# Prices, hops and search width of a static instruction planner in a four-layer graph network kernel

## The chip, the cores and the metric

The kernel runs on one core of one Trainium2 chip, in 32-bit floats. The metric is the device time of one execution in microseconds (us); the time before is 2462.25 us, the median of three runs (2461.93 to 2463.06). The engines are TensorE (PE, with its weight loads as PEld), VectorE (DVE), ScalarE (ACT), GpSimd (POOL) and SyncE (SP), each with its own queue of instructions that it works off in order.

## The reference

128 graphs of 64 nodes with 256 features pass through four layers. Each adds a graph layer's output to its input and normalises over the features:

```python
def _L0_gnn_ref(x, adj, mask, weight, w_ih, w_hh, b_ih, b_hh):    # gated graph layer, 5 rounds
    A = (adj != 0).astype(x.dtype)
    h = x
    for l in range(weight.shape[0]):
        m = jnp.einsum('bnd,de->bne', h, weight[l])
        agg = jnp.einsum('bij,bid->bjd', A, m)
        h = _gru_cell(agg, h, w_ih, w_hh, b_ih, b_hh)
    return h * mask[..., None]

def _L1_gnn_ref(x, adjacency, epsilon, W1, b1, rms_weight, W2, b2):
    agg = epsilon * x + jnp.einsum('bnm,bmd->bnd', adjacency, x)
    h = jnp.einsum('bnd,dh->bnh', agg, W1) + b1
    h = jax.nn.silu(_rmsnorm(h, rms_weight))
    return jnp.einsum('bnh,hd->bnd', h, W2) + b2

def _L2_gnn_ref(x, adj):                                          # on the hyperbolic ball
    x_tangent = logmap0(x)
    support_t = jnp.einsum('bij,bjd->bid', adj, x_tangent)
    return project(expmap0(support_t))

def _L3_gnn_ref(hidden, mask, W_w, W_b, a_w, a_b):                # attention
    h = jnp.einsum('bnd,ed->bne', hidden, W_w) + W_b
    ...
    return jnp.einsum('bnm,bmd->bnd', a, h)

x = _layernorm(x + _L0_gnn_ref(x, adj, nodemask, ...), axis=-1)
x = _layernorm(x + _L1_gnn_ref(x, adj, ...), axis=-1)
x = _layernorm(x + _L2_gnn_ref(x, adj), axis=-1)
x = _layernorm(x + _L3_gnn_ref(x, adj, ...), axis=-1)
```

## The kernel before

The work is cut into 16 groups of 8 graphs. A group's code does not emit its instructions at once: it hands each one to a planner, with the engine, an estimated duration (its price) and what it reads and writes. A group is one stream of operations. When all 16 are listed, the planner plays the engines against the prices and chooses in which order the operations of up to four streams go into each engine's queue; only that order reaches the chip. The prices themselves never do: on the chip each instruction starts when its engine is free and its inputs are there.

An operation as the planner holds it, and the step that advances one plan: it takes, again and again, the operation that can start first, and among equals the one a rule prefers. Marks `...` stand for cuts.

```python
    def advance(self, until, rank):
        flow, need, at, clock, banks = self.flow, self.need, self.at, self.clock, self.banks
        while self.left and clock["PE"] < until:
            best = None
            for s in range(self.first, min(self.first + flow.WINDOW, len(self.queues))):
                for e, q in self.queues[s].items():
                    opened = False
                    for _, o in zip(range(flow.AHEAD[e]), q):
                        t = max(clock[e], at[o.id])
                        if o.opens is not None:
                            if opened or not banks or need[o.id]:
                                opened = True
                                continue
                            t = max(t, banks[0])
                        elif need[o.id]:
                            continue
                        elif o.kb and e != "POOL":
                            t = max(t, self.lands[0])
                        key = (t, *rank(s, o))
                        if best is None or key < best[0]:
                            best = key, o
            if best is None:
                return False
            t, o = best[0][0], best[1]
            self.queues[o.stream][o.eng].remove(o)
            self.order.append(o)
            end = t + o.us
            clock[o.eng] = end
            if o.eng == "PE":
                self.done += o.us
            if o.opens is not None:
                banks.pop(0)
            for b in o.bufs:
                n = self.uses.get(b, b.left) - 1
                self.uses[b] = n
                if not n:
                    banks.append(end + flow.hop(o.eng, "PE"))
                    banks.sort()
            if o.kb:
                self.bus = max(self.bus, end + flow.DMA[0]) + o.kb / flow.DMA[1]
                end = self.bus + flow.DMA[2]
                if o.eng != "POOL":
                    self.lands = [*self.lands[1:], end]
            for u in o.then:
                need[u.id] -= 1
                at[u.id] = max(at[u.id], end + flow.hop(o.eng, u.eng))
            self.left -= 1
            while self.first < len(self.queues) and not any(self.queues[self.first].values()):
                self.first += 1
        return True

    def bound(self):

        now = self.clock["PE"]
        end = max(now - self.done + self.flow.work, *self.clock.values())
        for q in self.queues[self.first:]:
            for d in q.values():
                if d:
                    end = max(end, max(self.at[d[0].id], now) + d[0].way)
        return end
```

The rules of play, the hops (time from the end of an operation to the start of one that needs it on another engine) and the search over plans:

```python
    AHEAD = {"PE": 32, "DVE": 10, "ACT": 10, "POOL": 4, "SP": 2}
    HOPS = {"from PE": 0.25, "to PE": 0.3, "else": 0.1}
    DMA = (2.0, 330.0, 1.0)
    TRANSFERS = 8
    WINDOW, STRETCH, WIDTH, LAG = 4, 25.0, 8, 40.0
    ...
    def hop(self, e, to):
        if e == to:
            return 0.0
        return self.HOPS["from PE" if e == "PE" else "to PE" if to == "PE" else "else"]

    def ways(self):

        for i, o in enumerate(o for s in self.streams for o in s):
            o.id = i
        path = {}
        for ops in self.streams:
            longest = 0.0
            for o in reversed(ops):
                path[o] = o.us + max((path[u] + self.hop(o.eng, u.eng) for u in o.then if u.stream == o.stream), default=0.0)
                o.way = longest = max(longest, path[o])
        self.work = sum(o.us for ops in self.streams for o in ops if o.eng == "PE")

    def issue(self):
        self.ways()
        ranks = (lambda s, o: (s, o.n), lambda s, o: (s if o.kb else -s, o.n), lambda s, o: (self.LAG * s - o.way, s, o.n))
        plans, until = [Plan(self)], 0.0
        while any(p.left for p in plans):
            until += self.STRETCH
            found = {}
            for p in plans:
                for rank in ranks:
                    c = p.copy()
                    if c.advance(until, rank):
                        found.setdefault((round(c.bound(), 3), c.left), c)
            plans = [found[k] for k in sorted(found)[:self.WIDTH]]
        p, parts = plans[0], []
        past = (p.past, p.order)
        while past is not None:
            parts.append(past[1])
            past = past[0]
        ...   # the operations are emitted in the order of the best plan
```

The prices, by engine:

```python
    def pe(n, run, w, r):
        flow.op("PE", {512: 0.86, 256: 0.435, 128: 0.23, 1: 0.21}.get(n, 0.3), run, w, r)

    def turn(run, w, r):
        flow.op("PE", 0.11, run, w, r)

    def dve(n, run, w, r):
        flow.op("DVE", 0.16 + 0.00105 * n, run, w, r)

    def act(n, run, w, r):
        flow.op("ACT", 0.27 + 0.00077 * n, run, w, r)

    def pool(us, run, w, r=()):
        flow.op("POOL", us, run, w, r)
```

What the last groups do after their five gated rounds, cut to the operations that the profile shows at the end. The normalisation, used four times by each group:

```python
            st, mv = tiny("st", (P, NB, 6)), tiny("mv", (P, NB, 2))
            ve, rstd = tiny("ve", (P, 2, NB)), tiny("rstd", (P, 2, NB))
            for b in range(NB):
                dve(256, lambda b=b: nc.vector.bn_stats(st[:, b, :], y[:, b, :]), [(st, b)], [(y, b)])
                dve(4, lambda b=b: nc.vector.bn_aggr(mv[:, b, :], st[:, b, :]), [(mv, b)], [(st, b)])
            m = 2 if norm else 1
            dve(4, lambda: nc.vector.tensor_tensor(
                ve[:, :m, :], over(mv[:, :, 1], m), eps2[:, :m, :], OP.add), [ve], [mv])
            pool(1.1, lambda: nc.gpsimd.tensor_tensor(rstd[:, :m, :], ve[:, :m, :], pow2[:, :m, :], OP.pow), [rstd], [ve])
            if norm:
                dve(4, lambda: nc.vector.scalar_tensor_tensor(
                    norm.tile(), rstd[:, 1, :], float(np.sqrt(D)), rstd[:, 0, :], OP.mult, OP.mult), [norm], [rstd])
            o = rows(tag, f"x_{name}")
            off = tiny("off")
            dve(4, lambda: nc.vector.scalar_tensor_tensor(
                off.tile(), mv[:, :, 0], -1.0, rstd[:, 0, :], OP.mult, OP.mult), [off], [mv, rstd])
            for b in range(NB):
                if b % 2:
                    act(300, lambda b=b: nc.scalar.activation(
                        o[:, b, :], y[:, b, :], AF.Identity, bias=off[:, b:b + 1], scale=rstd[:, 0, b:b + 1]),
                        [(o, b)], [(y, b), off, rstd])
                else:
                    dve(240, lambda b=b: nc.vector.tensor_scalar(
                        o[:, b, :], y[:, b, :], mv[:, b, 0:1], rstd[:, 0, b:b + 1], OP.subtract, OP.mult),
                        [(o, b)], [(y, b), mv, rstd])
            return o
```

From the gated rounds to the second layer's output (the first line turns the state into rows; `ps_hid` and `ps_o1` are the two large products):

```python
        for n in range(2):
            ps = rows_of(hT, n)
            ...                                   # y0 = rows * nodemask + x
        x1 = layer_norm(y0, "A", "n0")
        for n in range(2):
            aggregate(aggm, x1, 2 * n, n)
        ...
        for c in range(KH):
            ps = bank("ps_hid")
            ...                                   # two 512-wide matmuls; hid and sq on ACT, sqs on DVE
        ps = bank("ps_ss")
        ...                                       # row sums of squares on PE, power on POOL, ps_rms on PE
        for c in range(KH):
            hc = hid[c]

            dve(512, lambda hc=hc, c=c: nc.vector.scalar_tensor_tensor(
                hc[0][:, hc[1], :], hc[0][:, hc[1], :], rmsc(c), ps_r.tile(), OP.mult, OP.mult), [hc], [hc, ps_r, cols])
            th = u("VZR"[c % 3], f"th{c}")
            act(512, lambda hc=hc, th=th: nc.scalar.activation(th.tile(), hc[0][:, hc[1], :], AF.Tanh, scale=0.5),
                [th], [hc])
            dve(512, lambda hc=hc, th=th: nc.vector.scalar_tensor_tensor(
                hc[0][:, hc[1], :], th.tile(), 1.0, hc[0][:, hc[1], :], OP.add, OP.mult), [hc], [hc, th])
        y1 = xb
        for h in range(NB // 2):
            ps = bank("ps_o1")
            ...                                   # 32 matmuls 256 wide for each half, y1 on DVE
        xn = tiny("n")
        x2 = layer_norm(y1, "A", "n1", xn)
```

The third and fourth layer:

```python
        ...
        act(2600, lambda: nc.scalar.activation(fac.tile(), fac.tile(), AF.Ln), [fac], [fac])
        ...                                       # a series of 9 small DVE operations, then the factor
        tan = rows("B", "tan")
        ...                                       # four scalings on DVE, ps_sup on PE, squares on ACT
        ...                                       # power on POOL, tanh on ACT, 6 small DVE operations
        x3 = layer_norm(y2, "B", "n2")
        for n in range(2):
            feats_of(x3T, x3, n)                  # ps_T: transposes on PE, copy on ACT
        ...                                       # ps_a: 258-wide matmuls, exp and scale on ACT
        ...                                       # ps_att on PE, four small steps each on DVE
        o = layer_norm(y3, "A", "n3")
        flow.op("SP", 0.1, lambda: nc.sync.dma_start(out_rows[g], o.tile()), (), [o])
```

## Time and profile before

| what | before |
|---|---|
| time, median of 3 runs | 2462.25 us |
| span of the profiled execution | 2460.1 us |
| TensorE busy | 2418.4 us (98%) |
| VectorE busy | 1708.3 us (69%) |
| ScalarE busy | 1232.9 us (50%) |
| GpSimd busy | 181.1 us (7%) |
| mean granted TensorE clock | 0.994 of full speed |
| data read and written | 24.69 and 8.39 MB |

The span runs from the first to the last instruction of one execution taken by the hardware profiler; the time of a run is some 2 us longer. An engine's busy time is the sum of the stretches in which it worked on at least one instruction; matmul ends are modelled, so a busy TensorE is not TensorE at its peak. A 32-bit matmul shows as two records. A wait line reads: engine, tile and line, what released it, then total us, how often, and the longest. In the order of time each row is a run of like instructions, with the idle time ahead of it in brackets.

### The profile page before, as it was taken

What the parts mean: (1) busy time and instruction counts of PE and PEld (TensorE: products, weight loads), DVE (VectorE), ACT (ScalarE), POOL (GpSimd) and SP (SyncE); (2) the same over time, 40 slices, a digit from 0 to 9 for tenths busy, and PEclk for the clock granted to TensorE, in tenths of its full rate; (3) what the DMA queues carried; (4) which work ended last, traced back from release to release, by engine and by line L of the source; (5) the groups of instructions that cost most, each with busy time, mean ns of one, the idle gap of its engine ahead of it and who ended that gap; (6) DMA issues with size and microseconds to landing.
All of it is one profiled execution on the core that took longest, in us unless ns stands there. A gap on an engine that the chain in (4) does not pass through costs nothing.

```text
span 2460.1 us, 31915 instructions
## 1 busy us (share of the span) xinstructions
PE 2418.4 (98%) x11922; PEld 2045.9 (83%) x11922; DVE 1708.3 (69%) x3741; ACT 1232.9 (50%) x2612; POOL 181.1 (7%) x144
## 2 busy tenths in 40 slices
PE   9999999999999999999999999999999999999995
PEld 7887887878788887888878788788888878878864
DVE  3656776767777766776776777677676767856776
ACT  3445455454545545454554544555554554454453
POOL 4000000000000000000000000000000000000011
PEclk9999999999999999999999999999999999999997
DMA  4000000000000000000000000000000000000000
GB/s 126 2 2 10 1 26 3 1 29 1 28 1 29 1 18 11 1 29 1 18 12 1 28 1 26 3 15 15 1 29 1 1 29 1 27 1 1 10 17 17
DMA packets 39145, 35.11 MB, mean 14 GB/s; under 512 B 9892, under 2 KB 38592, under 8 KB 38992
## 3 DMA queue, kind: packets, MB, share of 16 engines
q1 hardware_dynamic: 37264, 31.20, 4.0%
q8 instruction: 94, 1.54, 0.3%
q10 hardware_dynamic: 1328, 1.31, 0.2%
q0 software_dynamic: 400, 0.57, 0.1%
q14 instruction: 59, 0.48, 0.1%
HBM read 24.69 MB, written 8.39 MB: 13 GB/s over the span
## 4 chain that ended last, share of the span: by engine, by line
PE 73%; DVE 3%; ACT 1%; POOL 0%; issue 0%; POOLq 0%; ACTq 0%; DVEq 0%
PE p_v L625 9%; PE p_w L625 8%; PE p_r L625 8%; PE p_in L625 8%; PE p_hn L625 8%; PE ps_o L322 8%; PE ps_hid L322 8%; PE ps_agg L322 5%; PE p_u L625 4%; PE ps_hr L605 2%; PE ps_a L322 2%; PE ps_sup L322 1%; PE ps_att L322 1%; PE ps_T L595 1%; PE ps_ss L322 0%; DVE st L635 0%
## 5 line engine op out<-in xcount | busy, mean ns | idle before, releaser
L625 PE MATMUL p_hn<-hT,w_hn 128*128 128x256 f32 x1280 | 321.0, 380 | 0.1
L625 PE MATMUL p_in<-agg,w_in 128*128 128x256 f32 x1280 | 312.9, 380 | 0.0
L625 PEld LDWEIGHTS p_in<-agg,w_in 128*128 128x128 f32 x1280 | 241.5, 190 | 31.5 <-issue 0.5
L625 PEld LDWEIGHTS p_hn<-hT,w_hn 128*128 128x128 f32 x1280 | 229.4, 191 | 26.6 <-issue 2.6
L322 PE MATMUL ps_o<-w2s,hid 128*128 128x256 f32 x1024 | 230.0, 380 | 1.5 <-DVE hid L853 1.3
L322 PE MATMUL ps_hid<-aggm,w1s 128*128 128x512 f32 x512 | 224.1, 593 | 0.1
L322 PEld LDWEIGHTS ps_o<-w2s,hid 128*128 128x128 f32 x1024 | 194.3, 191 | 28.5 <-DVE hid L853 2.4
L640 POOL TENSOR_TENSOR rstd<-ve,pow 128x4 f32<-128x4 f32 (+1 forms) x64 | 81.9, 1280 | 1577.6 <-DVE ve L638 1569.3
L322 PEld LDWEIGHTS ps_hid<-aggm,w1s 128*128 128x128 f32 x512 | 96.7, 190 | 111.2 <-issue 108.3
L618 ACT COPY agg<-ps_agg 128x512 f32<-128x512 f32 x160 | 93.5, 584 | 149.2 <-PE ps_agg L322 123.1
L729 ACT ACTIVATE V<-V,half_b 128x256 f32<-128x256 f32 x160 | 73.0, 501 | 183.8 <-DVE V L725 183.7
L694 ACT ACTIVATE hnb<-p_hn,half_b 128x256 f32<-128x256 f32 x320 | 135.8, 471 | 55.7 <-PE p_hn L625 53.7
L625 PE MATMUL p_w<-tA,s 128*128 128x256 f32 x640 | 160.7, 380 | 0.0
L625 PE MATMUL p_v<-tB,s 128*128 128x256 f32 x640 | 159.5, 380 | 0.0
L625 PE MATMUL p_u<-tA,s 128*128 128x256 f32 x640 | 155.5, 380 | 1.5 <-DVE tA L708 1.4
L625 PE MATMUL p_w<-hT,s 128*128 128x256 f32 x640 | 156.7, 380 | 0.0
L625 PE MATMUL p_v<-tB,na 128*128 128x256 f32 x640 | 154.7, 380 | 0.7 <-DVE V L725 0.7
L625 PE MATMUL p_r<-hT,a 128*128 128x256 f32 x640 | 155.2, 380 | 0.2
L625 PE MATMUL p_r<-agg,a 128*128 128x256 f32 x640 | 154.1, 380 | 0.0
L833 DVE TENSOR_TENSOR sqs<-sqs,sq 128x512 f32<-128x512 f32 x112 | 77.4, 691 | 104.7 <-ACT sq L830 104.5
L322 PEld LDWEIGHTS ps_agg<-edge,hr 128*128 128x128 f32 x1024 | 137.3, 192 | 8.5 <-issue 1.4
L322 PE MATMUL ps_agg<-edge,hr 128*128 128x128 f32 x1024 | 139.1, 275 | 0.0
(205 smaller groups left out, 4435.3 us busy)
## 6 DMA issues: line engine op xcount, KB each, us to landing
x<-in_x_dram SPq DMA_DIRECT2D x16, 512.0 KB, 3.5
xr<-in_x_dram SPq DMA_DIRECT2D x16, 512.0 KB, 3.5
out_dram<-x_n SPq DMA_DIRECT2D x16, 512.0 KB, 2.9
edge<-in_adj_dram SPq DMA_DIRECT2D x32, 64.0 KB, 2.3
wm<-in_L_gnn_weight_dram SPq DMA_DIRECT2D x5, 256.0 KB, 4.9
w1s<-in_L_gnn_W_dram SPq DMA_DIRECT2D x1, 1024.0 KB, 6.3
w2s<-in_L_gnn_W_dram SPq DMA_DIRECT2D x1, 1024.0 KB, 10.0
aw_in_L_gnn_w_hh_dram<-in_L_gnn_w_hh_dram ACTq DMA_DIRECT2D x1, 512.0 KB, 5.6
```

What stands on the lines that cost most here:

```text
L322: return nc.tensor.matmul(o, lhsT, rhs, start=(k == 0), stop=(k == nk - 1))
L595: turn(lambda j=j, c=c: nc.tensor.transpose(ps[:, c * HR + j * P:c * HR + (j + 1) * P], src[:, 2 * n + j, c * P:(c + 1) * P], ident.tile() ...
L605: turn(lambda j=j, c=c: nc.tensor.transpose(ps[:, j * D + c * P:j * D + (c + 1) * P], src[:, c, (2 * n + j) * P:(2 * n + j + 1) * P], iden ...
L618: act(512, lambda: nc.scalar.copy(dst[:, :, half(n)], blocks_of(ps.tile())), [(dst, n)], [ps])
L625: pe(256, lambda c=c, k=k: nc.tensor.matmul(ps[:, c * HR:(c + 1) * HR], w[:, k, c * P:(c + 1) * P], v(k), start=first and c == k == 0, sto ...
L640: pool(1.1, lambda: nc.gpsimd.tensor_tensor(rstd[:, :m, :], ve[:, :m, :], pow2[:, :m, :], OP.pow), [rstd], [ve])
L694: act(300, lambda c=c: nc.scalar.activation(hnb[:, c, half(n)], p_hn[:, c * HR:(c + 1) * HR], AF.Identity, bias=half_b[:, 2 * KD + c:2 * K ...
L729: act(256, lambda c=c: nc.scalar.activation(o[:, c, :], src(c), AF.Tanh, bias=half_b[:, i * KD + c:i * KD + c + 1], scale=0.5), [(o, c)], ...
L833: dve(512, lambda sq=sq: nc.vector.tensor_add(sqs.tile(), sqs.tile(), sq.tile()), [sqs], [sqs, sq])
```

## The change

Only the planner's numbers and its search change. The prices of DVE, ACT and POOL operations are set anew, in good part per operation instead of by one formula, from durations seen in a trace. The hops become a part after the giving engine and a part before the taking one, and now also count between two dependent operations of one engine other than PE. An operation may hand over its result `early`, before its engine is free: the logarithm, whose price holds the reload of the tanh table that follows. In the last stretch of the span (`ENDGAME`, 350 us of planned TensorE work) the search goes in steps half as long and keeps three times as many plans. It is meant to make the planned course agree with the real one and to search the end more closely. The computation, the buffers and the transfers stay as they are.

```diff
-                at[u.id] = max(at[u.id], end + flow.hop(o.eng, u.eng))
+                at[u.id] = max(at[u.id], end + flow.hop(o, u.eng))
...   (cut)
-    HOPS = {"from PE": 0.25, "to PE": 0.3, "else": 0.1}
+    AFTER = {"PE": 0.2, "DVE": 0.12, "ACT": 0.13, "POOL": 0.04, "SP": 0.5}
+    BEFORE = {"PE": 0.1, "DVE": 0.0, "ACT": 0.0, "POOL": 0.05, "SP": 0.1}
+    ENDGAME = 350.0
...   (cut)
-    def op(self, eng, us, run, w=(), r=(), kb=0):
-        o = Op(eng, us, run, len(self.streams) - 1, len(self.ops), kb)
+    def op(self, eng, us, run, w=(), r=(), kb=0, early=0.0):
+        o = Op(eng, us, run, len(self.streams) - 1, len(self.ops), kb, early)
...   (cut)
-    def hop(self, e, to):
-        if e == to:
-            return 0.0
-        return self.HOPS["from PE" if e == "PE" else "to PE" if to == "PE" else "else"]
+    def hop(self, o, to):
+        return 0.0 if o.eng == to == "PE" else self.AFTER[o.eng] + self.BEFORE[to] - o.early
...   (cut)
-            until += self.STRETCH
+            late = until > self.work - self.ENDGAME
+            until += self.STRETCH / 2 if late else self.STRETCH
-            plans = [found[k] for k in sorted(found)[:self.WIDTH]]
+            plans = [found[k] for k in sorted(found)[:self.WIDTH * (3 if late else 1)]]
...   (cut)
-        flow.op("DVE", 0.16 + 0.00105 * n, run, w, r)
-    def act(n, run, w, r):
-        flow.op("ACT", 0.27 + 0.00077 * n, run, w, r)
+        flow.op("DVE", 0.075 + 0.00105 * n, run, w, r)
+    def act(us, run, w, r, early=0.0):
+        flow.op("ACT", us, run, w, r, early=early)
...   (cut)
-            act(512, lambda: nc.scalar.copy(dst[:, :, half(n)], blocks_of(ps.tile())), [(dst, n)], [ps])
+            act(0.49, lambda: nc.scalar.copy(dst[:, :, half(n)], blocks_of(ps.tile())), [(dst, n)], [ps])
...   (cut)
-            pool(1.1, lambda: nc.gpsimd.tensor_tensor(rstd[:, :m, :], ve[:, :m, :], pow2[:, :m, :], OP.pow), [rstd], [ve])
+            pool(1.65 if norm else 1.1, lambda: nc.gpsimd.tensor_tensor(rstd[:, :m, :], ve[:, :m, :], pow2[:, :m, :], OP.pow), [rstd], [ve])
...   (cut)
-                    act(300, lambda b=b: nc.scalar.activation(
+                    act(0.5, lambda b=b: nc.scalar.activation(
-                    dve(240, lambda b=b: nc.vector.tensor_scalar(
+                    dve(236, lambda b=b: nc.vector.tensor_scalar(
...   (cut)
-                    act(512, lambda: nc.scalar.copy(hr[:, 2 * n:2 * n + 2, :], blocks_of(ps.tile())),
+                    act(0.49, lambda: nc.scalar.copy(hr[:, 2 * n:2 * n + 2, :], blocks_of(ps.tile())),
-                    act(300, lambda c=c: nc.scalar.activation(
+                    act(0.375, lambda c=c: nc.scalar.activation(
...   (cut)
-                    act(256, lambda c=c: nc.scalar.activation(
+                    act(0.4, lambda c=c: nc.scalar.activation(
...   (cut)
-                    act(256, lambda c=c: nc.scalar.activation(t[:, c, :], t[:, c, :], AF.Tanh, bias=bih(2 * KD + c)),
+                    act(0.4, lambda c=c: nc.scalar.activation(t[:, c, :], t[:, c, :], AF.Tanh, bias=bih(2 * KD + c)),
...   (cut)
-            act(420, lambda: nc.scalar.copy(uu.tile(), blocks_of(p1.tile())), [uu], [p1])
+            act(0.49, lambda: nc.scalar.copy(uu.tile(), blocks_of(p1.tile())), [uu], [p1])
...   (cut)
-                dve(256, lambda ps=ps, b=b, j=j, blk=blk: nc.vector.scalar_tensor_tensor(
+                dve(300, lambda ps=ps, b=b, j=j, blk=blk: nc.vector.scalar_tensor_tensor(
...   (cut)
-            act(512, lambda ps=ps, hc=hc, c=c: nc.scalar.activation(
+            act(0.59, lambda ps=ps, hc=hc, c=c: nc.scalar.activation(
...   (cut)
-            act(512, lambda hc=hc, th=th: nc.scalar.activation(th.tile(), hc[0][:, hc[1], :], AF.Tanh, scale=0.5),
+            act(0.535, lambda hc=hc, th=th: nc.scalar.activation(th.tile(), hc[0][:, hc[1], :], AF.Tanh, scale=0.5),
...   (cut)
-        act(2600, lambda: nc.scalar.activation(fac.tile(), fac.tile(), AF.Ln), [fac], [fac])
+        act(2.67, lambda: nc.scalar.activation(fac.tile(), fac.tile(), AF.Ln), [fac], [fac], 1.28)
...   (cut)
-                act(450, lambda b=b, j=j, ps=sup[h]: nc.scalar.activation(
+                act(0.48, lambda b=b, j=j, ps=sup[h]: nc.scalar.activation(
-        act(64, lambda: nc.scalar.activation(th.tile(), unb.tile(), AF.Tanh), [th], [unb])
+        act(0.11, lambda: nc.scalar.activation(th.tile(), unb.tile(), AF.Tanh), [th], [unb])
...   (cut)
-        dve(800, onto_ball, [th, un], [th, un, urn])
+        dve(900, onto_ball, [th, un], [th, un, urn])
-            dve(256, lambda b=b, ps=sup[b // 2]: nc.vector.scalar_tensor_tensor(
+            dve(300, lambda b=b, ps=sup[b // 2]: nc.vector.scalar_tensor_tensor(
...   (cut)
-            act(4, lambda ps=ps, b=b: nc.scalar.activation(
+            act(0.17, lambda ps=ps, b=b: nc.scalar.activation(
-            act(256, lambda ps=ps, b=b: nc.scalar.activation(
+            act(0.38, lambda ps=ps, b=b: nc.scalar.activation(
...   (cut)
-            dve(256, lambda ps=ps, b=b: nc.vector.scalar_tensor_tensor(
+            dve(300, lambda ps=ps, b=b: nc.vector.scalar_tensor_tensor(
...   (cut)
```

## The prediction

> **What bounds the kernel now.** I read the page's busy table first, then the waits of TensorE (PE), then the busy time by stretches of the span, then the order of time at the end.
>
> ```profile
> span 2460.1 us, 31915 instructions
> PE 2418.4 (98%) x11922; PEld 2045.9 (83%) x11922; DVE 1708.3 (69%) x3741; ACT 1232.9 (50%) x2612; POOL 181.1 (7%) x144
> ```
>
> PE is busy for all but 2460.1 - 2418.4 = 41.7 us. No reordering of the same instructions can save more than these and what a lower clock costs. The waits of PE say what ended its idle time (total, times, longest, in us):
>
> ```profile
> PE ps_T L595 <- DVE x_n L654: 12.7, 2, 10.1
> PE ps_sup L322 <- DVE tan L900: 5.1, 1, 5.1
> PE ps_x L448 <- POOL ident masks.py:199: 2.5, 1, 2.5
> PE ps_ss L322 <- DVE sqs L833: 1.9, 1, 1.9
> ```
>
> These are single long waits, not many small ones. The stretches show where they lie (length, then busy us of PE, weight loads, DVE, ACT, POOL; then PE's granted clock, DMA share, GB/s):
>
> ```profile
> 800.00:1200.00 400.00, 399.01 (x1981) 339.78 (x1980) 284.21 (x614) 205.18 (x433) 24.17 (x18) 1.00 0.03 9
> 1200.00:1600.00 400.00, 400.00 (x1983) 339.01 (x1982) 283.10 (x601) 203.87 (x426) 25.22 (x18) 1.00 0.04 14
> 2300.00:2350.00 50.00, 50.00 (x240) 40.53 (x239) 39.86 (x91) 26.98 (x58) 5.61 (x3) 1.00 0.07 22
> 2350.00:2400.00 50.00, 43.42 (x170) 30.01 (x168) 34.58 (x82) 26.61 (x45) 7.38 (x5) 0.97 0.03 11
> 2400.00:2420.00 20.00, 14.14 (x59) 11.56 (x59) 15.19 (x53) 6.31 (x17) 3.21 (x3) 0.91 0.00 0
> 2420.00:2440.00 20.00, 9.47 (x36) 7.18 (x35) 16.63 (x74) 9.93 (x25) 2.63 (x3) 0.76 0.00 0
> 2440.00:2461.00 21.00, 8.36 (x32) 6.81 (x32) 8.75 (x34) 6.74 (x16) 2.01 (x2) 0.66 0.15 51
> ```
>
> From 2350 on PE is idle for 6.6 + 5.9 + 10.5 + 11.7 = 34.7 us (the last stretch is listed 0.9 us past the span's end). At the start it waits 2.5 us for the identity; the 2300 us between hold only some 4 us. So the middle is TensorE-bound almost without gaps, and the end is bound by the chain of small operations of the last two groups: PE has nothing else left to do. The order of time there, PE only (start, duration, what, idle before and its releaser):
>
> ```profile
> 2354.04 0.60 PE L605 MATMUL ps_hr<-ident,hT 128*128 128x128 f32 x4
> 2356.53 1.05 PE L322 MATMUL ps_ss<-ones,sqs 128*128 128x1 f32 x8 [1.89 <-DVE sqs L833]
> ...
> 2402.79 3.46 PE L322 MATMUL ps_sup<-tan,adjT 128*128 128x256 f32 x8 [5.10 <-DVE tan L900]
> ...
> 2428.46 1.47 PE L322 MATMUL ps_att<-hw,adjT 128*128 128x257 f32 x6
> 2440.01 1.94 PE L595 MATMUL ps_T<-ident,x_n 128*128 128x128 f32 x8 [10.08 <-DVE x_n L654]
> 2441.77 4.87 PE L322 MATMUL ps_a<-wattT,x3T 128*128 128x258 f32 x16
> 2446.47 1.90 PE L322 MATMUL ps_att<-hw,adjT 128*128 128x257 f32 x8
> ```
>
> The reader sees the last group alone from 2430 on: a hole of 10.1 us, three short pieces on PE, and from 2448.4 to 2460.1 no PE work at all (the last normalisation and the output transfer).
>
> **A floor.** Start-to-start in dense stretches gives PE's real work: 0.216 us for an instruction 256 wide (eight p_w in 1.73), 0.429 for 512, 0.111 for an aggregation of 128, 0.109 for a transpose. The groups by shape count 8616, 552, 1536 and about 1090 of these, and 128 of the sums' 0.1: 1861 + 237 + 170 + 119 + 13 = 2400 us. With 2.5 ahead of the first matmul and 11.7 behind the last, 2414 us is the least that any order gives; the span is 46 above it.
>
> **What the Trainium skill says.** "TensorE: Matmul & The Clock Gate", Part 1 (The HAM clock gate): after an idle window of about 3.4 us the array falls to half clock and needs as long a busy window to come back. The trace agrees: the clock column falls from 1.00 to 0.66, and sixteen ps_a take 4.87 us at the end where the chain of waits has 3.49 for sixteen at 1494.11. Holes thus cost twice, some 5 to 8 us in all; the planner's prices have no such term, before or after. "ScalarE: Activation LUTs", What ACT_TABLE_LOAD costs: 1283 ns for a load of a table set, plus a drain of about 1380 ns. The trace has sixteen loads of 1283 ns ahead of the logarithm, but no such drain: the logarithm starts 1.29 us after its load did (2398.63 and 2399.92). "VectorE: DVE Perf Modes", The DRAIN you can't avoid: an operation does not start until the pipe of the one before is empty. What I use of it is measured here: three dependent 4-wide operations start at 2397.97, 2398.16 and 2398.37 (0.2 apart), independent ones at 2397.17, 2397.25 and 2397.32 (0.08 apart).
>
> **The change part by part.** It neither adds nor removes an operation, a buffer or a transfer. All of it lies in the search that fixes the order of instructions, so PE's 2400 us stay.
> (a) *DVE prices.* A 512-wide operation goes from 0.16 + 0.538 = 0.698 to 0.613, a 4-wide from 0.164 to 0.079, but a dependent follower on the same engine now pays 0.12, before nothing. So 0.199 for a dependent small operation and 0.079 for an independent one: the 0.2 and 0.08 above. The planner now sees that two groups' chains interleave on DVE for nothing.
> (b) *ACT prices.* A 512-wide copy 0.664 to 0.49, a 256-wide tanh 0.467 to 0.40, the candidate's bias 0.501 to 0.375. The logarithm was 0.27 + 2.0 = 2.27 and then a hop; now its 2.67 hold the engine but the result leaves 1.28 earlier, after 1.39. In the trace it is out 1.5 us after its load began. That removes 0.9 us from each group's planned chain.
> (c) *POOL.* The 8-wide power 1.1 to 1.65; the trace has a mean of 1671 ns.
> (d) *Hops.* PE to DVE 0.25 to 0.20; DVE to PE 0.30 to 0.22. One handover in the trace: the hid operation starts at 2407.87, its 512 elements last 0.69, and PE starts at 2408.62: 0.75 after its start. The new price is 0.613 + 0.22 = 0.83, the old 0.698 + 0.30 = 1.00. Still on the safe side, so I expect no crop of small stalls in the middle: at most 2 us either way.
> (e) *The search.* In the last 350 us of planned PE work (from about 2050) it takes steps of 12.5 instead of 25 us and keeps 24 plans for 8. Each step tries three rules, so choices between the last groups are made twice as often from three times as many plans. This is the part that works where the idle time is.
>
> What can it win? The hole at 2354 to 2364 is 1.9 + 1.4 + 0.9 = 4.1 us. It has a cause in the order: half of the last group's ps_hr stands behind 13 us of the other group's ps_hid (2341.16 to 2354.04), though its inputs come some 5 us after p_in ended at 2335.5. Placed earlier, it puts that group's whole chain forward. I give 3 of the 4.1. Of the 5.1 at 2402.8, 2; of the 2.6 and 0.4 around 2419 to 2426, 1; of the 10.1 at 2440, 4, because the last group comes nearer to the one before and both share their holes. Less time at half clock gives 2. That is 12; the middle and new holes of the changed order give 1 back. 2462.25 - 11 = 2451.
>
> **Rivals.** *The end is a pure chain.* From the last ps_o (2416.7) to the end is 43 us with only some 10 us of dense PE work in it; a better order cannot shorten that. Then only the 4 us hole moves, and the time is 2458 to 2462. For it: DVE is busy 16.6 of 20 us at 2420 to 2440, so interleaving is not free there. Against: PE still works off the other group's ps_o until 2416, and the order decides whose. *Thinner margins.* Planned hops shrink by 0.05 to 0.17 us and the real machine stalls a little at many places: 16 groups of 5 layers with 0.05 to 0.1 us each are 4 to 8 us, which eats the win: 2455 to 2468. For it: PE's real 0.432 per matmul runs ahead of the planned 0.435. Against: (d). *A much better end.* Two groups side by side have 79 us of PE work from 2335.5 (each ps_hid 13.7, ps_o 13.8, and some 12 in small pieces), then 11.7: 2426 at the least. A search that came half-way there would give 2440. Against: the three rules are coarse, and nothing in them fills a hole on purpose.
>
> **Range and chances.** The middle of the pure chain is 2460, of my sum 2451, of the best search 2440. With most weight on the sum, 2442 to 2459 should hold eight in ten. Two per cent faster would be 2413, under the floor of 2414, so next to no chance. Two per cent slower needs 49 us of new idle time, more than the kernel has now: 0.01. I give nine in ten that it is faster at all.
>
> **What would show it.** Right: PE's busy time within 5 us of 2418, idle time after 2350 at 20 to 28 us, the wait of ps_T for x_n under 7 us, and the start and middle as now. Wrong: many waits of 0.1 to 0.5 us on PE between 100 and 2300 (thinner margins), or again a single hole of 8 us or more before the last ps_T with the same time (pure chain).

## The result: slower by 0.6 per cent

The changed kernel takes 2476.43 us (median of four runs, 2475.99 to 2476.65) against 2462.61 us for the kernel before in the same comparison: ratio 1.0056, interval 1.0039 to 1.0074. The prediction was 2451, with 2442 to 2459 as its range. The end of the span did become shorter, by what was predicted. The loss lies in the part where I had expected nothing.

The head of the page after the change:

```profile
span 2473.8 us, 31903 instructions
...
PE 2434.6 (98%) x11922; PEld 2030.6 (82%) x11922; DVE 1648.2 (67%) x3741; ACT 1230.0 (50%) x2610; POOL 181.5 (7%) x144
```

This is the first trap. PE has the same 11922 matmul records, yet its busy time rose by 16.2 us and its idle time fell, from 41.7 to 39.2 us, in a kernel that is 13.7 us longer. A matmul record of 256 columns is 0.38 us long, where such matmuls start 0.216 apart; its modelled end reaches 0.16 us into whatever follows. A delay shorter than that leaves no idle time on the page. The Trainium skill warns of matmul busy time in "Perfetto Trace Analysis", Identifying the Most-Contended Engine: it is no good measure of how close a kernel is to its limit, and the busy share of the weight loads is one to use in its place. Here that share moved the right way, from 83 to 82% (2045.9 to 2030.6 us).

The waits of PE after the change (total us, times, longest):

```profile
PE ps_hr L609 <- DVE hT L754: 6.8, 8, 1.4
PE ps_sup L326 <- DVE tan L904: 6.0, 2, 3.7
PE ps_T L599 <- DVE x_n L658: 4.8, 1, 4.8
PE ps_x L452 <- POOL ident masks.py:199: 2.5, 1, 2.5
PE p_u L629 <- DVE tA L712: 2.1, 8, 0.6
PE p_v L629 <- DVE tB L712: 1.5, 3, 0.9
```

The wait of ps_T for x_n fell from 12.7 to 4.8 us, so the long hole at the end is halved. In the gated rounds in the middle ps_hr and p_u now wait eight times each, and p_v's waits for tB are new. Before the change there were three such waits in all for hT and tA:

```profile
PE p_u L625 <- DVE tA L708: 1.4, 1, 1.4
PE ps_hr L605 <- DVE hT L750: 1.4, 2, 1.0
```

How much is missing there shows in the stretches, by the number of matmul records in brackets after PE's busy time:

```profile
800.00:1200.00 400.00, 397.86 (x1945) 330.95 (x1944) 267.19 (x603) 206.71 (x434) 25.77 (x19) 1.00 0.03 10
1200.00:1600.00 400.00, 396.72 (x1943) 330.77 (x1942) 277.77 (x644) 203.69 (x428) 28.38 (x20) 1.00 0.04 14
...
2400.00:2420.00 20.00, 20.00 (x93) 16.13 (x92) 16.95 (x32) 9.54 (x16) 1.01 (x1) 1.00 0.00 1
2420.00:2440.00 20.00, 14.43 (x63) 11.75 (x62) 12.46 (x69) 6.38 (x16) 4.37 (x3) 0.88 0.00 0
```

PE is 99% busy from 800 to 1200, but does 1945 records where it did 1981.

**A measure that sees short delays.** From the trace I took the distance from each matmul's start to the next one's and subtracted the dense spacing of its shape (0.216 us for 256 to 258 columns, 0.429 for 512, 0.1115 for an aggregation, 0.109 for a transpose, 0.101 for a row sum). What is left I call the excess. The dense work is 2400.6 us in every kernel, so start (before 20 us), middle (20 to 2300) and end (from 2300 to the last instruction) add up to the span but for rounding:

| kernel | start | middle | end | span |
|---|---|---|---|---|
| before | 6.1 | 8.7 | 44.6 | 2460.1 |
| changed | 6.5 | 36.0 | 30.8 | 2473.8 |

The end won 13.8 us, the middle lost 27.3. In the middle 224 starts came more than 20 ns late, against 43 before; 178 of the 224 were under 0.164 us late and so leave no idle time.

**Where one delay comes from.** The order of time of the changed kernel, around one gated round (start, duration, what, idle before and its releaser):

```profile
1027.12 0.69 DVE L712 TENSOR_TENSOR tA<-ps_agg,agg 128x512 f32<-128x512 f32 x1 [0.27 <-PE ps_agg L326]
1027.84 0.58 ACT L622 COPY agg<-ps_agg 128x512 f32<-128x512 f32 x1
...
1028.46 0.69 DVE L712 TENSOR_TENSOR tB<-hT,ps_agg 128x512 f32<-128x512 f32 x1 [0.65 <-ACT agg L622]
...
1029.07 0.69 DVE L748 TENSOR_TENSOR hT<-hT,R 128x512 f32<-128x512 f32 x1
...
1029.20 1.13 PE L629 MATMUL p_v<-tB,s 128*128 128x256 f32 x4
1029.67 0.68 DVE L712 TENSOR_TENSOR tA<-hT,tA 128x512 f32<-128x512 f32 x1
...
1030.50 0.89 PE L629 MATMUL p_u<-tA,s 128*128 128x256 f32 x3 [0.17 <-DVE tA L712]
```

Three operations read the bank ps_agg (a part of PSUM, where the results of TensorE land): VectorE, ScalarE, VectorE. Each starts when the one before it has ended, though all three only read: in the trace the copy carries a wait for VectorE's semaphore and the second read one for ScalarE's, so the program keeps them apart. VectorE stands still for 0.65 us, everything behind it in its queue comes as much later, and p_u starts late. The view shows 0.17 us of that, but p_v starts at 1029.20 and has four records, 0.86 us dense, before p_u at 1030.50: 1.30, so 0.44 us are lost. The planner has no such rule. It orders a read after a write, but two reads of one bank are free of each other. The Trainium skill gives a reason for such waits, "PSUM — Partial Sum Buffer", PSUM bank collisions raise a hardware error: accesses of two engines to one bank in the same partitions have to be kept apart, reads against reads included. The trace agrees: of the changed kernel's 80 first reads, paired with the nearest copy by start time, 2 overlap it by more than 50 ns, and none does if each copy is used only once.

### The profile page after: what moved, and what is told of

Its sections match the earlier page's. It is cut to its first block, busy times and chain, and to the rows that moved or that the text cites. A ratio compares the mean times of both kernels' runs of the same rounds, so it can differ in the third digit from the quotient of the medians.

```text
span 2473.8 us, 31903 instructions
## 1 busy us (share of the span) xinstructions
PE 2434.6 (98%) x11922; PEld 2030.6 (82%) x11922; DVE 1648.2 (67%) x3741; ACT 1230.0 (50%) x2610; POOL 181.5 (7%) x144
## 4 chain that ended last, share of the span: by engine, by line
PE 81%; DVE 8%; ACT 2%; issue 1%; POOL 1%; POOLq 0%; ACTq 0%; DVEq 0%
PE p_r L629 10%; PE p_in L629 9%; PE ps_o L326 9%; PE ps_hid L326 9%; PE p_w L629 9%; PE p_v L629 9%; PE p_hn L629 8%; PE ps_agg L326 5%; PE p_u L629 4%; PE ps_hr L609 2%; PE ps_a L326 2%; PE ps_sup L326 1%; PE ps_T L599 1%; PE ps_att L326 1%; DVE hT L754 1%; DVE tA L712 1%
## 5 line engine op out<-in xcount | busy, mean ns | idle before, releaser
L629 PE MATMUL p_w<-tA,s 128*128 128x256 f32 x640 | 154.5, 379 | 0.0
L742 DVE SCALAR_TENSOR_TENSOR R<-R,hnb 128x512 f32<-128x512 f32 x80 | 59.4, 743 | 136.8 <-ACT R L733 136.5
L629 PEld LDWEIGHTS p_u<-tA,s 128*128 128x128 f32 x640 | 117.5, 190 | 29.3 <-issue 7.3
```

The source lines that it names most:

```text
L629: pe(256, lambda c=c, k=k: nc.tensor.matmul(ps[:, c * HR:(c + 1) * HR], w[:, k, c * P:(c + 1) * P], v(k), start=first and c == k == 0, sto ...
L742: dve(512, lambda: nc.vector.scalar_tensor_tensor(t.tile(), t.tile(), 1.0, hnb[:, :, half(n)], OP.add, OP.mult), [t], [t, (hnb, (n, 0)), ( ...
```

## The experiments

Two theories. **Bank:** the planner does not know that readers of a bank follow each other, and the old prices hid it. **Margin:** planned handovers to TensorE are too tight everywhere, by 0.1 us or so, for many small reasons. A third, that the new search is to blame, comes first. In the table the time is the median of the runs; start-to-start distances are those of one profiled execution. The last three columns are parts of the middle, by the tile whose matmul was late.

| run | time | ratio (interval) | middle | end | p_u + p_v | ps_hr | ps_o |
|---|---|---|---|---|---|---|---|
| before | 2462 | 1 | 8.7 | 44.6 | 4.3 | 1.9 | 0.0 |
| changed | 2476.43 | 1.0056 (1.0039-1.0074) | 36.0 | 30.8 | 18.7 | 8.7 | 4.2 |
| search_alone | 2455.37 | 0.9971 (0.9960-0.9983) | 7.9 | 39.9 | 3.6 | 1.8 | 0.0 |
| prices_alone | 2485.78 | 1.0095 (1.0080-1.0110) | 35.9 | 41.1 | 20.1 | 8.1 | 4.3 |
| bank_order | 2454.69 | 0.9966 (0.9953-0.9979) | 15.6 | 29.3 | 2.5 | 6.5 | 3.7 |
| margin10 | 2460.91 | 0.9995 (0.9986-1.0003) | 21.4 | 30.9 | 8.0 | 6.9 | 1.9 |
| act_only | 2460.62 | 0.9993 (0.9984-1.0002) | 8.7 | 42.9 | 3.4 | 0.2 | 0.1 |
| dve_hops_only | 2472.66 | 1.0041 (1.0026-1.0056) | 25.6 | 37.8 | 9.7 | 7.1 | 3.8 |
| control_after | 2467.30 | 1.0019 (1.0012-1.0026) | 27.7 | 31.2 | 11.8 | 5.6 | 3.5 |
| bank_xb | 2452.77 | 0.9959 (0.9945-0.9974) | 10.7 | 33.5 | 2.4 | 2.1 | 2.9 |
| after_xb | 2464.79 | 1.0009 (1.0002-1.0016) | 25.4 | 30.8 | 15.6 | 1.1 | 4.8 |
| bank_margin10 | 2457.65 | 0.9981 (0.9972-0.9990) | 16.0 | 31.6 | 5.1 | 4.3 | 1.6 |
| bank_xb_hid | 2448.30 | 0.9946 (0.9930-0.9962) | 9.3 | 34.0 | 3.6 | 1.9 | 0.3 |
| combined | 2446.30 | 0.9935 (0.9917-0.9952) | 9.3 | 28.6 | 3.5 | 1.9 | 0.4 |

### Search alone, prices alone

The first is the kernel before with this; the second is the changed kernel with `ENDGAME = -1e9`, so that the search never narrows its steps.

```diff
-            until += self.STRETCH
+            late = until > self.work - self.ENDGAME
+            until += self.STRETCH / 2 if late else self.STRETCH
-            plans = [found[k] for k in sorted(found)[:self.WIDTH]]
+            plans = [found[k] for k in sorted(found)[:self.WIDTH * (3 if late else 1)]]
```

> The kernel before with its old prices and hops, and of the change the search alone (half steps and three times the plans in the last 350 us). Sum of what TensorE's starts lie apart beyond the dense spacing, from 20 to 2300 us: 8.7 us before, 36.0 us after the change. If the new prices are the cause of the loss (both the bank theory and the margin theory): this sum stays at 7 to 12 us, idle time after 2350 falls below 30 us, and the time is 2448 to 2458. If the new search is the cause: 2466 or more.

> The changed kernel with all its new prices and hops, but the old search to the end (steps of 25 us, 8 plans). Bank and margin theory alike: the sum between 20 and 2300 stays at 30 to 40 us, the end is longer than with the new search, and the time is 2474 to 2484, slower than the change as a whole. If the new search were the cause: 2462 or less.

The search alone gave 2455.37 us with a middle of 7.9: it wins 6.6 us and harms nothing. The prices alone gave 2485.78, a little above what was expected, with the whole loss in the middle (35.9). So the search is cleared. The middle belongs to prices and hops, the end to both: 44.6 falls by 4.7 with the search, by 3.5 with the prices, by 13.8 with the two together.

### The shared bank told to the planner

Prices, hops and search of the change; a second reader on another engine is planned behind the first.

```diff
+                        for b in o.bufs:
+                            held = self.held.get(b)
+                            if held and held[0] != e:
+                                t = max(t, held[1] + flow.BEFORE[e])
...
+                if o.eng != "PE":
+                    self.held[b] = (o.eng, end + flow.AFTER[o.eng])
```

> The changed kernel, and the planner knows one thing more: where ScalarE and VectorE read the same PSUM bank, the second starts only after the first has ended plus its hop. Prices, hops and search as in the change. Bank theory (the machine lets the two readers of one bank follow each other, the planner thought them free to run at once, so what TensorE waits for comes 0.6 us later than planned): the waits of tA and tB for agg nearly vanish on the path to TensorE, the sum between 20 and 2300 falls from 36 to 18 to 25 us, the time is 2456 to 2464. Margin theory: the sum stays over 30 and the time within 4 us of 2476.

2454.69 us and a middle of 15.6, both better than the bank theory had said, and far from the margin theory's 30. The views of waits with tA, tB or agg, of the changed kernel and then of this one (the lines in which VectorE and ScalarE wait for each other over them):

```profile
DVE tA L712 <- ACT agg L622: 41.5, 26, 9.0
...
DVE tB L712 <- ACT agg L622: 10.7, 16, 0.9
...
ACT agg L622 <- DVE tA L712: 3.3, 8, 0.7
...
ACT agg L622 <- DVE tB L712: 1.9, 4, 0.7
```

```profile
ACT agg L629 <- DVE tA L719: 2.5, 6, 0.9
...
ACT agg L629 <- DVE tB L719: 2.2, 4, 0.8
...
DVE tA L719 <- ACT agg L629: 0.9, 2, 0.5
```

In the kernel before, it was mostly ScalarE that waited for VectorE:

```profile
DVE tA L708 <- PE ps_agg L322: 49.0, 32, 11.8
...
ACT agg L618 <- DVE tA L708: 24.8, 40, 1.3
...
DVE tA L708 <- ACT agg L618: 5.1, 7, 1.2
```

The new prices turned that round, and with the bank rule VectorE's 52.2 us of waiting for the copy (41.5 and 10.7) fall to 0.9. Not all of the 52.2 is due to the bank. A wait counts all the idle time ahead of an operation, the longest is 9.0 us where a copy takes 0.58, and before the change the same operation stood 49.0 us for the product itself (6.8 after). At 0.65 us for each of the 42 waits, the copy's own part is an estimated 27 us. By start times the planner now lets VectorE read twice and ScalarE copy last in about 29 of 80 cases (7 in the changed kernel), and mixes the two engines in about 7 (26). The same prices that lost 14 us now win 7.3 (2461.99 for the kernel before in that comparison). From 800 to 1200 PE does 1963 records, against 1945:

```profile
800.00:1200.00 400.00, 398.43 (x1963) 336.36 (x1962) 272.53 (x633) 204.09 (x433) 24.81 (x19) 1.00 0.04 11
```

### Slack instead of knowledge

```diff
-    BEFORE = {"PE": 0.1, "DVE": 0.0, "ACT": 0.0, "POOL": 0.05, "SP": 0.1}
+    BEFORE = {"PE": 0.2, "DVE": 0.0, "ACT": 0.0, "POOL": 0.05, "SP": 0.1}
```

> The changed kernel with 0.1 us more on every hop to TensorE (0.20 for 0.10), nothing else. Margin theory (planned handovers to TensorE are simply too tight): the sum between 20 and 2300 falls from 36 to under 15 us and the time is 2448 to 2456. Bank theory: the slack covers only a part of a 0.6 us delay; the sum is 18 to 28 us and the time 2458 to 2468.

2460.91 us and 21.4, inside what the bank theory allowed. Slack of 0.1 us does buy back more than half of the loss, without knowing its cause; p_u and p_v keep 8.0 us of it, where the bank rule leaves 2.5.

### Which prices

Both start from the kernel before with its old search. In the first only ScalarE's prices are new, in the second only VectorE's prices and the hops.

```diff
-    def act(n, run, w, r):
-        flow.op("ACT", 0.27 + 0.00077 * n, run, w, r)
+    def act(us, run, w, r, early=0.0):
+        flow.op("ACT", us, run, w, r, early=early)      # act_only, with the new price at each call
-        flow.op("DVE", 0.16 + 0.00105 * n, run, w, r)
+        flow.op("DVE", 0.075 + 0.00105 * n, run, w, r)  # dve_hops_only, with AFTER and BEFORE
```

> The kernel before with the new ScalarE prices alone; VectorE and GpSimd prices, hops and search are the old ones. More of the copies of agg now stand ahead of VectorE's first reader of the same bank (44 of 80 against 35 before and 50 after the change). If that order alone makes the loss: the sum of TensorE's excess between 20 and 2300 us is 20 us or more and the time 2470 or more. If the old VectorE prices and hops hold enough slack to cover a reader that comes 0.6 us late: the sum stays at 7 to 13 us and the time at 2457 to 2464.

> The kernel before with the new VectorE prices and the new hops; ScalarE and GpSimd prices and the search are the old ones. If the loss is the thin slack alone: the sum between 20 and 2300 us is near that of the whole change, 28 to 36 us, and the time 2474 to 2486. If it takes both (thin slack and the ScalarE copy ahead of VectorE on the shared bank): the sum is 10 to 22 us and the time 2458 to 2472.

ScalarE's prices alone change nothing (2460.62, middle 8.7), though they do put more copies first (44 of 80 for 35, by the order in the queues). With new VectorE prices and hops the middle is 25.6 and the time 2472.66: more than "it takes both" had allowed (10 to 22), less than the slack alone (28 to 36), so neither expectation fits. VectorE waits for the copy only 6.7 us in this run (5.1 before, 52.2 in the changed kernel), so most of this loss is not the bank's order. prices_alone, which has the new ScalarE and GpSimd prices as well, loses 10.3 us more in the middle, all of it before p_u and p_v (9.7 to 20.1), and there VectorE waits 53.9 us for the copy. So the thin slack does most of the loss, and the ScalarE prices, harmless by themselves, probably bring the bank in on top of it; the step of 10 us is not far above what one plan differs from another, as the next run shows.

### Is it one unlucky plan?

```diff
-    WINDOW, STRETCH, WIDTH, LAG = 4, 25.0, 8, 40.0
+    WINDOW, STRETCH, WIDTH, LAG = 4, 25.0, 8, 41.0
```

> The changed kernel with one unrelated number of the search moved a little (LAG 41 for 40), so that other plans are chosen from the same prices. It shows how far the loss is an accident of one plan. Bank theory: again 28 to 40 us between 20 and 2300, again 20 to 24 us less than before in the end after 2300 is possible or not, and the time is 2466 to 2482. If the loss is an accident of the plan: under 2462.

2467.30 us, as expected, middle 27.7, just under the 28 expected, end 31.2. The loss stays and is smaller by 8 us. So the 36.0 has a part that belongs to this plan; differences of a few us in one kernel's middle should not be given to a cause from one plan alone.

### What was left: GpSimd beside VectorE

In bank_order ps_hr still has 6.5 us. One such case in its order of time:

```profile
790.45 2.36 POOL L826 TENSOR_TENSOR xb<-x_n,b_r 128x1024 f32<-128x1024 f32 x1 [1.46 <-DVE hT L759]
790.95 2.40 DVE L761 SCALAR_TENSOR_TENSOR hT<-hT,R 128x512 f32<-128x512 f32 x1
...
793.50 0.63 PE L616 MATMUL ps_hr<-ident,hT 128*128 128x128 f32 x4 [1.22 <-DVE hT L761]
```

A VectorE operation that takes 0.69 us elsewhere takes 2.40 beside the addition of b2 on GpSimd, and ends 0.54 us after it. Such a hold (a VectorE operation over 0.25 us longer than is usual for its kind) stands beside 11 of the 16 additions in the kernel before, and beside 12 of 16 after. The skill names a possible cause, "GPSIMD Engine Reference", 1. Specifications: GpSimd shares its SBUF interfaces with VectorE, with contention when VectorE has two SBUF inputs (SBUF holds all tiles of the kernel that are not in PSUM). The held operations have two. The trace agrees, as the changed kernel's order of time shows at another addition:

```profile
502.07 2.37 POOL L819 TENSOR_TENSOR xb<-x_n,b_r 128x1024 f32<-128x1024 f32 x1 [1.81 <-DVE Z L742]
502.15 0.69 DVE L744 TENSOR_TENSOR Z<-p_in,Z 128x512 f32<-128x512 f32 x1
...
503.97 1.03 DVE L748 TENSOR_TENSOR hT<-hT,Z 128x512 f32<-128x512 f32 x1 [1.13 <-ACT Z L746]
```

Z<-p_in,Z has one source in PSUM and lasts its usual 0.69 us in the midst of the addition; hT<-hT,Z has both in SBUF and ends 0.55 us after it. I counted the VectorE operations that start beside an addition (at most 0.2 us ahead of it) and share at least 0.15 us with it: in the kernels before and after, 23 of 25 with two SBUF sources are over 0.2 us longer than the median of their kind, and none of the 23 others; in the ten kernels that keep the addition on GpSimd it is 107 of 122 and 1 of 101. The experiment moves the addition to VectorE:

```diff
-        pool(2.4, lambda: nc.gpsimd.tensor_tensor(xb.tile(), x1.tile(), over(b2_r.tile(), NB), OP.add), [xb], [x1, b2_r])
+        dve(1030, lambda: nc.vector.tensor_tensor(xb.tile(), x1.tile(), over(b2_r.tile(), NB), OP.add), [xb], [x1, b2_r])
```

> As bank_order, and the addition of b2 (xb, 2.4 us on GpSimd for each group) goes to VectorE, priced at 1.16 us. Port theory: VectorE operations with two SBUF sources that start beside the GpSimd addition last until 0.55 us after its end (2.4 us for 0.69) and hold back ps_hr; then the long VectorE operations vanish, ps_hr's part of the sum falls from 6.5 to under 3 us, the sum between 20 and 2300 from 15.6 to 9 to 13, and the time is 2447 to 2453. If 16 more VectorE operations cost more than the hold: 2455 or more.

> The changed kernel, and only the addition of b2 goes from GpSimd to VectorE (price 1.16 us); the planner still knows nothing of shared banks. Port theory: the part of ps_hr in the sum falls from 8.8 to under 5 us and no VectorE operation of 512 elements lasts over 2 us any more; the parts of p_u and p_v stay near 18 us, the sum is 29 to 33 us and the time 2467 to 2474. If the hold at the port is of no weight: ps_hr stays over 7 us and the time within 3 us of 2476.

With the bank rule ps_hr falls from 6.5 to 2.1 and the middle to 10.7, but the time only to 2452.77, not clearly apart from bank_order's 2454.69, as the end of this plan is 4.2 us longer. Without the bank rule, on the changed kernel, ps_hr falls from 8.7 to 1.1 and p_u + p_v stay at 15.6: the two causes are apart. The middle of 25.4 and the time of 2464.79 are lower than expected; 3.1 of the surplus are in p_u + p_v and fit the scatter of plans. The mean of the held operations (busy us and mean ns after the count), in the changed kernel and in after_xb:

```profile
L754 DVE SCALAR_TENSOR_TENSOR hT<-hT,R 128x512 f32<-128x512 f32 x80 | 63.8, 798 | 2.2
```

```profile
L754 DVE SCALAR_TENSOR_TENSOR hT<-hT,R 128x512 f32<-128x512 f32 x80 | 55.1, 689 | 2.0
```

### More slack on top, a last price, and all together

> As bank_order, with 0.1 us more on every hop to TensorE as well. If what is left of the sum after bank_order (15.6 us, most of it before ps_hr and ps_o) is thin slack: it falls to 7 to 11 us and the time to 2447 to 2453. If it is the hold of VectorE by GpSimd, 2 us at a time: ps_hr's 6.5 us stay over 4.5, only ps_o's 3.7 fall under 2, and the time is 2451 to 2456.

bank_order with the 0.1 us of margin10 gave 2457.65 and a middle of 16.0. It fits neither expectation: ps_hr (4.3) and ps_o (1.6) fell, and p_u rose to 4.2, 2.7 and 1.2 of it in two late starts of a different plan. In this plan the slack saved nothing on top of the bank rule; more than that the run does not say.

The small delays before ps_o come from one price. The scaling of hid reads one source in PSUM; in the changed kernel's trace such operations start 0.658 us apart when they follow each other, the new formula has 0.613 (the old one 0.698).

```diff
-            dve(512, lambda hc=hc, c=c: nc.vector.scalar_tensor_tensor(
+            dve(560, lambda hc=hc, c=c: nc.vector.scalar_tensor_tensor(
```

> As bank_xb, with the price of the hid scaling on VectorE (one source in PSUM) at 0.663 for 0.613 us, as its starts lie apart in the trace (0.658). If the small waits before ps_o come from this price: their part of the sum falls from 2.9 to under 1.5 us, the sum to 8 to 10, and the time to 2448 to 2453, with the end of the span as the larger uncertainty. If not: ps_o stays over 2.3 us.

2448.30 us, ps_o 0.3, middle 9.3: that the small waits come from this price is shown. How much time it saves is not: the profiled execution took 2451.97 us where the other three took 2448.10 to 2448.50, and its middle and end together are only 0.9 us shorter than bank_xb's. The last run adds a closer search of the end.

```diff
-    ENDGAME = 350.0
+    ENDGAME = 200.0
-            until += self.STRETCH / 2 if late else self.STRETCH
+            until += self.STRETCH / 4 if late else self.STRETCH
-            plans = [found[k] for k in sorted(found)[:self.WIDTH * (3 if late else 1)]]
+            plans = [found[k] for k in sorted(found)[:self.WIDTH * (12 if late else 1)]]
```

> As bank_xb_hid, with steps of 6.25 us and 96 plans in the last 200 us. Sum between 20 and 2300 as there, 8 to 10 us. If the end still profits from a closer search: excess after 2300 at 24 to 28 us (29.3 in bank_order and 33.5 in bank_xb, counted to the end of the span) and the time 2443 to 2450. If the end is now a pure chain: 2450 to 2454.

2446.30 us, 0.9935 of the kernel before (0.9917 to 0.9952), and faster than both kernels of this case. The middle is as full as before, with the new prices:

```profile
800.00:1200.00 400.00, 399.92 (x1986) 340.19 (x1985) 278.86 (x643) 207.44 (x441) 19.68 (x17) 1.00 0.04 12
```

Its end, 28.6, is just above the 24 to 28 that were expected. What is left of it is a chain; PE in order of time:

```profile
2403.14 3.65 PE L333 MATMUL ps_sup<-tan,adjT 128*128 128x256 f32 x8 [2.31 <-DVE tan L911]
2410.24 3.56 PE L333 MATMUL ps_sup<-tan,adjT 128*128 128x256 f32 x8 [3.44 <-DVE tan L911]
2418.60 1.97 PE L606 MATMUL ps_T<-ident,x_n 128*128 128x128 f32 x8 [4.80 <-DVE x_n L665]
...
2432.21 1.90 PE L333 MATMUL ps_att<-hw,adjT 128*128 128x257 f32 x8
```

The last two groups now run side by side, so each hole is short, and both ps_sup run at about half the dense rate (eight in 3.6 us, 1.73 dense).

## Why the prediction was wrong

- **The end (step e and the sum of 12): right.** Idle time after 2350 is 123.8 - 101.0 = 22.8 us, within the 20 to 28 named; the wait of ps_T is 4.8, under 7; the excess of the end fell by 13.8. The search's part is shown by itself: 4.7 us without the new prices, 10.3 with them (41.1 to 30.8). That the total fits is in part luck. The waits of ps_T fell by 7.9 us where the sum took some 5 off, the 4.1 us of short waits behind ps_hid became 1.5 (0.85 at 2384 and 0.67 at 2388) where it took 3 off, and the waits of ps_sup rose by 0.9 where it took 2 off.
- **Step (d) failed: "Still on the safe side, so I expect no crop of small stalls in the middle: at most 2 us either way."** It was 27.3. The handover that I looked at was read rightly: in the changed kernel, too, p_v starts 0.74 us after the VectorE operation that it needs (1028.46 to 1029.20), and the new price says 0.83. But I judged a plan by one handover. What made PE late was that VectorE's operation itself started later than planned, for reasons that the planner does not hold. The old prices were too long and thereby held slack for at least three such things: the bank's readers, the hold beside GpSimd, the slower read from PSUM. Making the prices true took away the slack and left the three.
- **The sizes of the three**, from the table: the bank rule takes 20.4 us off the middle, the move of the addition 4.9, the hid price 1.4. That is 26.7 of the 27.3, in this order; the move alone took 10.6 (after_xb). The first size carries the scatter of plans that control_after shows (8 us), and the step from dve_hops_only to prices_alone puts it nearer to 10.
- **The rival "thinner margins"** named the place and the kind and gave 4 to 8 us, by counting rounds times 0.05 to 0.1. It was mis-sized: 27 us, since the delays reach from under 0.1 to 1.6 us and are more than one to a round (some 150 of the 224 in 80 rounds, and 55 before ps_o). It also took price and hop together for the hop: 0.17 us is what both lose, and the hops between TensorE and VectorE or ScalarE lose 0.05 to 0.08. I set the rival aside by (d).
- **The signs.** "PE's busy time within 5 us of 2418" was missed by 16 and did show that something was wrong, but I had read it as work, not as hidden delays. "Many waits of 0.1 to 0.5 us" was right in substance; PE's view of waits shows only a few of them. From 20 to 2300 PE's idle time is 2280 - 2266.5 = 13.5 us of the 36.0.
- **The start** was as before (6.1 and 6.5), and two per cent either way was rightly ruled out.
- **VectorE's small operations.** What the prediction quotes of the skill, that an operation does not start until the pipe of the one before is empty, does not show in its three independent operations: they start 0.08 us apart while the record of the first lasts 0.17. The prices rest on the measured distances, so nothing hangs on this.

Open: what makes most of the 25.6 us in dve_hops_only was not traced, no two runs differ in the sources of a held VectorE operation alone (the count above stands in for that), and the 9.3 us of the combined kernel's middle were not followed up.

## What to carry to other kernels

When a planner's estimates are made true, list first what it does not model at all (engines that take turns on a memory bank or hold each other at the memory), since estimates that were too long may have been paying for it; put the rule in before the slack goes. Judge a TensorE-bound stretch by start-to-start distances or by the number of records in a window, not by busy or idle time. And try a change of search and a change of prices each alone: here one won 0.3% and the other lost 1%.

## What the runs showed of the hardware

The hold of VectorE beside a GpSimd addition was not expected: 11 of the 16 additions before the change and 12 after it stretch a VectorE operation, in most cases one of 0.69 us, to as much as 2.85 us, and most of these end 0.55 us after the addition. Of the operations with at most one source in SBUF, 1 of 101 was held (a tensor_scalar on edge in bank_order, 2.01 us for 0.29). An engine that is 7% busy thus delayed TensorE by 4 to 8 us in all, once nothing hid it (ps_hr from 6.5 to 2.1 and from 8.7 to 1.1 without the addition). And two readers of one PSUM bank cost some 0.65 us of waiting where the reading engine changes and has nothing else to do, since the program keeps them apart.
